# The value product of the last attention layer turned round, and the planner's lengths refreshed

## The chip, the cores and the metric

The kernel runs on one core of a Trainium2 chip. The metric is the device time of one execution in microseconds (us); the time of a kernel is the median of several executions. A profile is one more execution, recorded by the hardware. The engines have short names in it: PE is TensorE (matmuls; PEld its weight loads), DVE is VectorE, ACT is ScalarE, POOL is GpSimd, SP is the queue that issues DMAs. Everything here is float32 except the masks, which are bfloat16.

## The reference

A batch is a graph of 512 nodes with 256 features; there are 32 batches and one 512x512 adjacency matrix for all. Four layers follow one another, each of the form `x = x + layer(relu(layernorm(x)))`:

- layer 0: an MLP of width 512, graph attention without a mask (512 wide), a second MLP, graph attention with the adjacency mask (256 wide);
- layer 1: graph attention, mask with the diagonal added;
- layer 2: a transformer block with eight-head attention and the mask;
- layer 3: graph attention with four heads of 64 features, which is the layer that changes:

```python
q = (h @ W).reshape(B, N, H, D)                    # H = 4, D = 64
e = e_src[:, :, None, :] + e_dst[:, None, :, :]
e = jnp.where(e >= 0, e, ALPHA * e)
e = jnp.where(mask, e, NEG_INF)
attn = jax.nn.softmax(e, axis=2)                   # over the neighbours j
h_prime = jnp.einsum('bijh,bjhd->bihd', attn, q)
return jax.nn.elu(h_prime.reshape(B, N, H * D))
```

A node without neighbours has the same score for all nodes, so its row of `h_prime` is the mean of `q`.

## The kernel before

**Tiling.** A batch's 512 nodes are four blocks (`NC`) of 128 partitions; a feature map is either nodes first (128 partitions x 4 blocks x 256) or transposed, channels first (128 partitions x 2 x 512). Whole batches are the unit of parallel work: up to `IN_FLIGHT` = 4 of them are open, each with one of four "x" buffers that it holds from the load of its input to the store of its output.

**Order.** Nothing runs in program order. Each batch (`Graph`) first states its work as operations: an engine, a length in us, buffers read and written, and a function that issues the instructions. `Plan.order` (L158) then goes through all operations of all batches like a simulator of the five engines: it places next the operation that can start first, and among those that can start at the same time the one with the earliest due time, which is the batch's number times `PERIOD` less the length of what follows it in the batch. The result is one fixed order per engine; each engine executes its queue strictly in that order, and waits where an operand isn't there. The lengths thus decide the order and nothing else; a wrong length doesn't cost time by itself, but puts an instruction ahead of another that would have been ready sooner. `HOP` and `DRAIN` (L124) are added between engines.

**Buffers.** Work buffers are 28 of the kind "cell" (one feature map, or half of an attention matrix: two of its four 128-row blocks), 9 of the kind "row" (128 x 522) and eight PSUM banks (128 x 512). The planner assigns them as it goes, and `safe` (L231) refuses to hand one out where some batch could then not finish.

**Graph attention** is the same for all layers, in `gat_probabilities` (L587). The score is built transposed: neighbours j on the partitions, nodes i along the columns. TensorE spreads a column of node terms over all partitions by transposing it (`rows_ps`, L576); VectorE takes the masked maximum (L609) and two small steps on four columns (L618, L627, L628); TensorE and ScalarE make a row of the result (L576, L584); GpSimd adds the transposed mask to that row, two blocks at a time (L643, 128x1024); VectorE takes the maximum of the two slopes of the leaky ReLU (L655); and ScalarE takes the exponential (L663). The result p is two cells, unnormalized.

**Layer 3** is `layer3` (from L1239). `nodes_first` (L560) computes q and the 16 columns of node terms; ScalarE copies q into a cell where each head has 64 features and a 65th column that GpSimd sets to one (L1271). `lonely` (L669) computes the mean for nodes without neighbours and puts it, or zero, into y. Then each head by itself gets its p, and the value product of L1290: for each block c of 128 nodes, p's 128x128 block is loaded as the weights, and 128 columns of q that include the head's 65 stream through, four matmuls in a chain; the 65th column gives the sum of the row. VectorE clamps and inverts the sums (L1303, L1304) and adds the scaled 64 columns into y (L1306, one instruction per block). At the end ELU and the addition to x (L707, L711, L720, L1034).

The MHA of layer 2 (`mha`, L1136) already has a value product of another shape (L1206): the values are the weights, 32 columns for each of four heads, each head at its own quarter of the PSUM partitions, and p transposed streams through; the result, channels first, is copied to a row (L1219) and turned by two transposes (L1227).

Of the kernel before, what the change touches and what calls it, by code (L numbers as in the profile page):

```python
# [115 lines left out]
class Plan:  # L116
# [9 lines left out]

    def __init__(self):
        self.ops = []
        self.writers = {}
        self.readers = {}  # L130

    def add(self, graph, engine, length, reads, writes, emit, lag):
        op = Op()
        op.engine, op.length, op.emit, op.graph, op.lag = engine, length, emit, graph, lag
# [174 lines left out]
def adj_preln_kernel(  # L309
# [116 lines left out]
    def weight(w):  # L426
        return held("w", name_of[id(w)])
# [7 lines left out]
    class Graph:  # L435
# [29 lines left out]
        def normalized(self, src, func, n):  # L465
# [5 lines left out]
            for c in range(NC):  # L471
# [8 lines left out]
                "dve", 0.3, [mv], [var], lambda: dve.tensor_add(var.ap, mv[:, :, 1], eps)  # L480
            )
            self.op(
                "pool", 1.21, [var], [rstd],
# [3 lines left out]
                "dve", 0.25, [mv, rstd], [off],  # L487
# [41 lines left out]
        def channels_first(self, src, w, cols, dst, bias=None):  # L529

            nk = w.shape[1]
            for m in range(2 * len(dst)):
                mm = Buffer("bank", N)
                for k in range(nk):
                    s, i = src[k // 2], k % 2
                    self.op(
                        "pe", 0.92, [s.part(i)] if k else [*src, weight(w)],
# [16 lines left out]
        def nodes_first(self, src, w, cols, n, c, mm, dst):  # L554
# [13 lines left out]
            self.op("pe", 0.435 * nk, [*src, weight(w), terms(w)], [mm, dst], emit)  # L568
# [18 lines left out]
        def gat_probabilities(self, holder, term, n, bias=None, biasT=None, own=False, after=()):  # L587
# [10 lines left out]
            if bias is None:  # L598
# [5 lines left out]
                self.op("dve", 1.6, [f2_ps, *holder], [top, s], emit)  # L604
            else:
                for c in range(NC):
                    self.op(
                        "dve", 0.79, [f2_ps, held("mask", c)], [top],
                        lambda c=c: dve.tensor_tensor_reduce(  # L609
                            masked, f2_ps.ap, bias[:, c, :], 1.0, LOWEST,  # L610
                            op0=ALU.add, op1=ALU.max, accum_out=top[:, c : c + 1],
                        ),
                    )
# [8 lines left out]
                self.op("dve", 0.65 if own else 0.5, [top, *holder], [top, s], emit)  # L622
# [9 lines left out]
            self.op("dve", 0.8, [s, *holder], [m, w], emit)  # L632
# [36 lines left out]
        def lonely(self, v, n, y, split):  # L669
# [7 lines left out]
            self.op("pool", 1.94, [v], [add], emit)  # L677
# [23 lines left out]
        def elu(self, y, parts, shape, twice=False):  # L701
# [4 lines left out]
                "dve", 0.9 if big else 0.51, [parts], [e],  # L706
# [207 lines left out]
        def layer0(self):  # L914
# [30 lines left out]
            for i in range(2):  # L945
                self.op(
                    "pool", 1.38, [p[i]], [sums.part(i)],
# [20 lines left out]
            for m in range(KH):  # L968
# [17 lines left out]
                if i:  # L986
                    self.elu(lambda y=y: y.ap, y.part(), (2, N), twice=True)
                    self.op(
                        "pool", 2.35, [y, r1T[m // 2]], [y],
# [11 lines left out]
            for g in range(2):  # L1001
# [5 lines left out]
                def emit(g=g, tp=tp):  # L1007
# [10 lines left out]
                    "dve", 1.3, [tp, part], [part],  # L1018
# [3 lines left out]
                    "dve", 0.85, [xt.part(2 * g, 2), part], [xt.part(2 * g, 2)],  # L1022
# [97 lines left out]
        def pair_first(self, src, w, cols, c, mm, i, dst):  # L1120
# [13 lines left out]
            self.op("pe", 0.435 * nk + 0.07, [src, weight(w)], [mm.part(i), dst], emit)  # L1134

        def mha(self, g, qT, kT, v, y):  # L1136
# [7 lines left out]
            for c0 in range(0, NC, 2):  # L1144
                pT = [Buffer("cell", NC, 2, P) for _ in range(PACK)]
                for c in (c0, c0 + 1):
# [17 lines left out]
                    self.op("pe", 1.2, reads, [*sc, *p], emit)  # L1164
                    for h in range(PACK):
# [3 lines left out]
                            "dve", 0.83, [sc[h], held("mask", c)], [half, low],  # L1169
# [46 lines left out]
                self.op("pe", 2.1, [v, reads], [acc, r, valued], emit)  # L1216
# [23 lines left out]
                self.op("dve", 0.7, [back, sums], [rinv, y], emit)  # L1240

        W3 = GAT_DIM + 1

        def layer3(self):
            w3 = self.W3
            xn = self.normalized(self.xt, AF.Relu, 1)
            hT = self.transposed(xn)
            q = Buffer("cell", NC, GAT_HEADS * w3)
            f = self.small("f16", NC, TERMS, GAT_HEADS)
            n = C + TERMS * GAT_HEADS  # L1250

            def heads_of(ap):
                return ap.rearrange("p (h d) -> p h d", h=GAT_HEADS)

            for c in range(NC):
# [3 lines left out]
                def emit(c=c, mm=mm):  # L1259
# [3 lines left out]
                    act.activation(  # L1263
                        heads_of(q[:, c, :])[:, :, :GAT_DIM], heads_of(mm[:, :C]), AF.Copy
                    )

                self.op("act", 0.57, [mm], [f, q.part(c)], emit)

            def emit():
                ones_at = q.ap.rearrange("p c (h d) -> p (c h) d", h=GAT_HEADS)  # L1270
                pool.memset(ones_at[:, :, GAT_DIM:], 1.0)  # L1271

            self.op("pool", 0.13, [], [q], emit)
            y = Buffer("cell", NC, C)
            self.lonely(q, GAT_HEADS * w3, y, GAT_HEADS)
            after = []
            for h in range(GAT_HEADS):
                p, top = self.gat_probabilities(
                    [f], lambda t, h=h: f[:, :, t, h], h % 2, mask_bias, mask_biasT, False, after
                )  # L1280
                after = [top]

                first = min(h * w3, GAT_HEADS * w3 - P)
                at = h * w3 - first
                mm = Buffer("bank", NC, P)
                for c in range(NC):

                    def emit(c=c, p=p, mm=mm, first=first):
                        for j in range(NC):
                            pe.matmul(  # L1290
                                mm[:, c, :],
                                p[j // 2][:, j % 2, c * P : (c + 1) * P],
                                q[:, j, first : first + P],
                                start=(j == 0),
                                stop=(j == NC - 1),
                            )

                    self.op("pe", 1.02, [q, y.part(c), *p], [mm], emit)
                rinv = self.small(f"rinvh{h % 2}", NC, 1)

                def emit(h=h, mm=mm, rinv=rinv, at=at):
                    hs = slice(h * GAT_DIM, (h + 1) * GAT_DIM)
                    dve.tensor_max(rinv.ap, mm[:, :, at + GAT_DIM : at + w3], tiny[:, :, None])  # L1303
                    dve.reciprocal(rinv.ap, rinv.ap)  # L1304
                    for c in range(NC):
                        dve.scalar_tensor_tensor(  # L1306
# [76 lines left out]
```

## Time and profile before

Three executions took 5247.51, 5250.43 and 5252.19 us, so the median is 5250.43. The profiled execution took 5251.43 us; its span, from the first to the last instruction, is 5249.7 us.

| engine | busy, us | share of the span | instructions |
|---|---|---|---|
| PE (matmul) | 4933.7 | 94% | 28816 |
| PEld (weight loads) | 3494.5 | 67% | 28816 |
| DVE | 3652.2 | 70% | 9752 |
| ACT | 3389.3 | 65% | 7173 |
| POOL | 2222.0 | 42% | 1487 |

The rows of the parts that change:

| line, what | count | mean, ns |
|---|---|---|
| L1290 PE matmul record, 128x128 (two records make one float32 matmul) | 4096 | 282 |
| L1303 DVE clamp, 128x4 | 128 | 157 |
| L1304 DVE reciprocal, 128x4 | 128 | 178 |
| L1306 DVE scale and add, 128x64 | 512 | 277 |
| L1263 ACT copy of q, 128x256 | 128 | 382 |
| L1271 POOL ones, 128x16 | 32 | 127 |
| L643 POOL mask addition, 128x1024 | 320 + 64 | 2151, 2195 |
| L990 POOL addition, 128x1024 | 64 | 2476 |
| L948 POOL addition, 128x512 | 64 | 1284 |

A matmul's recorded length includes the time in which its last columns run out of the array while the next one already streams, so records overlap and their lengths don't add up; a transpose of 128x128 is one record. The granted TensorE clock is 0.98 of full speed over the span. DMA moves 45.58 MB in all and is busy only at the start (weights) and at each batch's load and store.

### The profile page before, as it was taken

How to read it: one execution, taken by the hardware profiler on the slowest of the kernel's cores; microseconds unless marked ns; L12 is line 12 of the kernel's file. 1: busy time of each engine (PE TensorE's matmuls, PEld its weight loads, DVE VectorE, ACT ScalarE, POOL GpSimd, SP SyncE). 2: the span in 40 equal slices, each digit the busy share in tenths (PEclk: the TensorE clock that was granted, in tenths of full speed). 3: DMA queues.
4: the chain of work that ended last, by engine and by line, in shares of the span. 5: the costliest groups of instructions: out<-in, count | busy, mean ns of one | idle time of the engine just before them, and what ended most of it. 6: DMA issues, size and time to landing. Idle time of an engine off the chain costs nothing.

```text
span 5249.7 us, 78394 instructions
## 1 busy us (share of the span) xinstructions
PE 4933.7 (94%) x28816; PEld 3494.5 (67%) x28816; DVE 3652.2 (70%) x9752; ACT 3389.3 (65%) x7173; POOL 2222.0 (42%) x1487
## 2 busy tenths in 40 slices
PE   8999999999999999999999999999999999999987
PEld 5666666676666666766666666666666666666565
DVE  5576667677767766677667767677676767767677
ACT  4656666666667666666656666666766666657774
POOL 2244444354433444343444434444344443343355
PEclk9999999999999999999999999999999999999997
DMA  2000000000000000000000000000000000000000
GB/s 70 1 9 1 9 9 9 9 9 1 9 9 9 9 1 9 9 9 9 9 1 9 9 9 9 1 9 9 9 9 1 9 9 9 9 1 9 1 5 13
DMA packets 40624, 45.58 MB, mean 9 GB/s; under 512 B 2992, under 2 KB 38320, under 8 KB 40240
## 3 DMA queue, kind: packets, MB, share of 16 engines
q1 hardware_dynamic: 38624, 40.57, 2.4%
q8 instruction: 227, 3.72, 0.3%
q14 instruction: 157, 1.29, 0.1%
q10 hardware_dynamic: 1616, 0.01, 0.0%
HBM read 23.80 MB, written 16.78 MB: 8 GB/s over the span
## 4 chain that ended last, share of the span: by engine, by line
PE 70%; DVE 18%; ACT 7%; POOL 3%; issue 2%; DMA 0%; DVEq 0%; POOLq 0%; ACTq 0%
PE bank L560 14%; PE bank L539 10%; PE bank L751 8%; PE bank L975 8%; PE bank L1290 7%; PE bank L1188 6%; PE bank L576 4%; PE bank L1206 3%; DVE masked L609 3%; PE bank L1151 3%; PE bank L1126 3%; DVE cell L655 2%; PE bank L511 2%; DVE smalls L627 2%; ACT cell L1178 1%
## 5 line engine op out<-in xcount | busy, mean ns | idle before, releaser
L643 POOL TENSOR_TENSOR cell<-mask_biasT,row 128x1024 f32<-128x1024 bf16 x320 | 681.3, 2151 | 604.0 <-ACT row L584 587.9
L1178 ACT ACTIVATE cell<-cell,smalls 128x512 f32<-128x512 f32 x1024 | 733.9, 717 | 273.1 <-DVE smalls L1170 270.2
L1170 DVE CUSTOM_DVE_ANT_0 cell<-bank,mask_bias 128x512 f32<-128x512 f32 x1024 | 684.3, 682 | 182.4 <-PE bank L1151 180.8
L609 DVE CUSTOM_DVE_ANT_0 masked<-bank,mask_bias 128x512 f32<-128x512 f32 x768 | 529.4, 689 | 395.6 <-PE bank L576 371.8
L1197 ACT ACTIVATE cell<-bank 128x512 f32<-128x512 f32 x1024 | 578.3, 593 | 218.8 <-PE bank L1188 214.6
L1188 PE MATMUL bank<-ident,cell 128*128 128x128 f32 x4096 | 588.1, 278 | 91.7 <-ACT cell L1178 49.7
L1188 PEld LDWEIGHTS bank<-ident,cell 128*128 128x128 f32 x4096 | 471.2, 142 | 261.7 <-ACT cell L1178 116.5
L1290 PEld LDWEIGHTS bank<-cell,cell 128*128 128x128 f32 x4096 | 517.4, 196 | 93.0 <-issue 65.1
L1290 PE MATMUL bank<-cell,cell 128*128 128x128 f32 x4096 | 562.4, 282 | 15.0 <-ACT cell L663 8.6
L751 PE MATMUL bank<-cell,cell 128*128 128x261 f32 x2048 | 502.0, 397 | 27.9 <-ACT cell L663 16.3
L663 ACT ACTIVATE cell<-cell,smalls 128x512 f32<-128x512 f32 x640 | 427.1, 715 | 124.7 <-DVE cell L655 123.8
L539 PE MATMUL bank<-cell,mlp_sb 128*128 128x512 f32 x1024 | 485.9, 604 | 4.3 <-ACT cell L519 3.5
L484 POOL TENSOR_TENSOR smalls<-smalls,neg_half 128x4 f32<-128x4 f32 x192 | 205.8, 1072 | 662.6 <-DVE smalls L480 495.5
L751 PEld LDWEIGHTS bank<-cell,cell 128*128 128x128 f32 x2048 | 392.2, 196 | 135.7 <-ACT cell L663 39.7
L560 PE MATMUL bank<-fc_sb,cell 128*128 128x256 f32 (+1 forms) x2048 | 480.6, 382 | 0.9 <-ACT cell L1197 0.2
L975 PE MATMUL bank<-cell,cell 128*128 128x512 f32 x1024 | 459.9, 594 | 0.0
L1034 POOL TENSOR_TENSOR x<-x,cell 128x512 f32<-128x512 f32 x192 | 259.8, 1365 | 465.8 <-DVE cell L720 426.4
L576 PE MATMUL bank<-ident,smalls 128*128 128x128 f32 x2304 | 355.2, 281 | 71.6 <-DVE smalls L628 54.4
L560 PEld LDWEIGHTS bank<-fc_sb,cell 128*128 128x128 f32 x2048 | 376.8, 191 | 59.0 <-issue 6.1
L655 DVE SCALAR_TENSOR_TENSOR cell<-bank,smalls,cell 128x512 f32<-128x512 f32 x512 | 356.2, 745 | 46.4 <-POOL cell L643 39.6
L576 PEld LDWEIGHTS bank<-ident,smalls 128*128 128x128 f32 x2304 | 270.4, 140 | 174.3 <-issue 93.4
L496 ACT ACTIVATE cell<-x,smalls 128x256 f32<-128x256 f32 x512 | 269.6, 590 | 142.8 <-DVE smalls L488 142.5
(131 smaller groups left out, 8871.9 us busy)
## 6 DMA issues: line engine op xcount, KB each, us to landing
x<-in_x_dram SPq DMA_DIRECT2D x32, 512.0 KB, 3.7
out_dram<-x SPq DMA_DIRECT2D x32, 512.0 KB, 3.0
mlp_sb<-in_L_gnn_mlp_w_dram SPq DMA_DIRECT2D x2, 512.0 KB, 6.6
fc_sb<-in_L_gnn_W_fc_dram SPq DMA_DIRECT2D x1, 1024.0 KB, 7.7
row<-in_adj_dram SPq DMA_DIRECT2D x4, 256.0 KB, 7.4
qkv_sb<-in_L_gnn_w_qkv_dram SPq DMA_DIRECT2D x1, 768.0 KB, 7.5
cell<-in_L_gnn_a_fc_dram SPq DMA_DIRECT2D x1, 512.0 KB, 6.3
l_sb<-in_L_gnn_W_dram SPq DMA_DIRECT2D x2, 256.0 KB, 5.9
```

The lines of the kernel that those rows point to most:

```text
L539: lambda k=k, s=s, i=i, m=m, mm=mm: pe.matmul(mm.ap, w[:, k, cols + m * P : cols + (m + 1) * P], s[:, i, :], start=(k == 0), stop=(k == nk ...
L560: pe.matmul(mm[:, :n], src[k // 2][:, k % 2, c * P : (c + 1) * P], w[:, k, cols : cols + n], start=(k == 0), stop=(k == nk - 1),)
L576: pe.transpose(bc[:, c * P : (c + 1) * P], col(c).to_broadcast([P, P]), ident)
L609: lambda c=c: dve.tensor_tensor_reduce(masked, f2_ps.ap, bias[:, c, :], 1.0, LOWEST, op0=ALU.add, op1=ALU.max, accum_out=top[:, c : c + 1],),
L643: lambda half=half: pool.tensor_add(p[half].ap, biasT[:, 2 * half : 2 * half + 2, :], w_row[:, None, :].to_broadcast([P, 2, N]),),
L751: pe.matmul(mm[:, :w1], p[j // 2][:, j % 2, c * P : (c + 1) * P], v[:, j, :], start=(j == 0), stop=(j == NC - 1),)
L975: pe.matmul(mm.ap, h1[jh][:, i, m * P : (m + 1) * P], p[jh][:, i, :], start=(jh + i == 0), stop=(jh + i == 2),)
L1170: lambda h=h, c=c, sc=sc, p=p: dve.tensor_tensor_reduce(p[h // 2][:, h % 2, :], sc[h].ap, mask_bias[:, c, :], -MHA_SCALE, HIGHEST, op0=ALU ...
L1178: lambda h=h, c=c, p=p: act.activation(p[h // 2][:, h % 2, :], p[h // 2][:, h % 2, :], AF.Exp, scale=-1.0, bias=low[:, c, h : h + 1], accu ...
L1188: pe.transpose(tp[:, j, :], p[h // 2][:, h % 2, j * P : (j + 1) * P], ident)
L1197: lambda h=h, c=c, tp=tp, pT=pT: act.activation(pT[h][:, :, c % 2, :], tp.ap, AF.Copy),
L1290: pe.matmul(mm[:, c, :], p[j // 2][:, j % 2, c * P : (c + 1) * P], q[:, j, first : first + P], start=(j == 0), stop=(j == NC - 1),)
```

## The change

Layer 3's heads are taken in pairs. q's 64 columns of a head become the weights, the first head of a pair on columns 0 to 63 of the array and the second on 64 to 127, and p streams through as it lies, all 512 nodes at once; the result is channels first (two heads x 64 on the partitions, nodes along the columns). The ones column goes; GpSimd adds the four blocks of each head's p to one 128x512 map instead (an addition of 128x1024, then one of 128x512), and a product with 32 columns of ones per head sums these over the partitions, the four heads at the four quarters of one bank. ScalarE copies each of the three banks to a row, TensorE turns each by four transposes, VectorE clamps and inverts the sums and multiplies, two heads at a time, into a new cell z. y, the part of the nodes without neighbours, is added last, in two halves. A head's value product no longer waits for y.

Apart from this, some twenty of the planner's lengths are set to other values, and the planner gets a new term, `OVERLAP`: operations of ScalarE and VectorE keep their engine for 0.115 and 0.07 us less than their length, and that time is added to the delay with which their result counts as there.

```diff
+    OVERLAP = {"act": 0.115, "dve": 0.07}
...
-        op.engine, op.length, op.emit, op.graph, op.lag = engine, length, emit, graph, lag
+        over = self.OVERLAP.get(engine, 0.0)
+        op.engine, op.length, op.lag = engine, length - over, lag + over
+        op.emit, op.graph = emit, graph
...
-                "pool", 1.21, [var], [rstd],
+                "pool", 1.07, [var], [rstd],
...
-                        "pe", 0.92, [s.part(i)] if k else [*src, weight(w)],
+                        "pe", 0.88, [s.part(i)] if k else [*src, weight(w)],
...
-            self.op("pe", 0.435 * nk, [*src, weight(w), terms(w)], [mm, dst], emit)
+            self.op("pe", 0.45 * nk, [*src, weight(w), terms(w)], [mm, dst], emit)
...
-                        "dve", 0.79, [f2_ps, held("mask", c)], [top],
+                        "dve", 0.77, [f2_ps, held("mask", c)], [top],
...
-                    "pool", 1.38, [p[i]], [sums.part(i)],
+                    "pool", 1.7, [p[i]], [sums.part(i)],
...
-                    "dve", 1.3, [tp, part], [part],
+                    "dve", 0.77, [tp, part], [part],
...
-            self.op("pe", 0.435 * nk + 0.07, [src, weight(w)], [mm.part(i), dst], emit)
+            self.op("pe", 0.43 * nk + 0.04, [src, weight(w)], [mm.part(i), dst], emit)
...
-                    self.op("pe", 1.2, reads, [*sc, *p], emit)
+                    self.op("pe", 1.14, reads, [*sc, *p], emit)
...
-                            "dve", 0.83, [sc[h], held("mask", c)], [half, low],
+                            "dve", 0.77, [sc[h], held("mask", c)], [half, low],
...
-                self.op("pe", 2.1, [v, reads], [acc, r, valued], emit)
+                self.op("pe", 1.97, [v, reads], [acc, r, valued], emit)
...
-                self.op("dve", 0.7, [back, sums], [rinv, y], emit)
+                self.op("dve", 1.0, [back, sums], [rinv, y], emit)
...
-            q = Buffer("cell", NC, GAT_HEADS * w3)
+            q = Buffer("cell", NC, C)
...
-                pool.memset(ones_at[:, :, GAT_DIM:], 1.0)
...
-            self.lonely(q, GAT_HEADS * w3, y, GAT_HEADS)
+            self.lonely(q, C, y, 1)
...
-                            pe.matmul(
-                                mm[:, c, :],
-                                p[j // 2][:, j % 2, c * P : (c + 1) * P],
-                                q[:, j, first : first + P],
-                                start=(j == 0),
-                                stop=(j == NC - 1),
-                            )
-
-                    self.op("pe", 1.02, [q, y.part(c), *p], [mm], emit)
...
-                    dve.tensor_max(rinv.ap, mm[:, :, at + GAT_DIM : at + w3], tiny[:, :, None])
-                    dve.reciprocal(rinv.ap, rinv.ap)
...
-                        dve.scalar_tensor_tensor(
-                            y[:, c, hs], mm[:, c, at : at + GAT_DIM], rinv[:, c, :], y[:, c, hs],
-                            op0=ALU.mult, op1=ALU.add,
-                        )
...
+                    halves = Buffer("cell", 2, N)
+                    self.op(
+                        "pool", 2.4, p, [halves],
+                        lambda p=p, halves=halves: pool.tensor_add(halves.ap, p[0].ap, p[1].ap),
+                    )
+                    self.op(
+                        "pool", 1.27, [halves], [total.part(i)],
+                        lambda i=i, halves=halves, total=total: pool.tensor_add(
+                            total[:, i, :], halves[:, 0, :], halves[:, 1, :]
+                        ),
+                    )
...
+                acc = Buffer("bank", N)
+                r = Buffer("row", N)
+                for half in range(2):
+
+                    def emit(g=g, ps=ps, acc=acc, half=half):
+                        for k in range(2):
+                            for i in range(2):
+                                d = (2 * g + i) * GAT_DIM
+                                pe.matmul(
+                                    acc[i * GAT_DIM : (i + 1) * GAT_DIM, :],
+                                    q[:, 2 * half + k, d : d + GAT_DIM],
+                                    ps[i][half][:, k, :],
+                                    start=(half + k == 0),
+                                    stop=(half + k == 2),
+                                )
+
+                    self.op("pe", 1.78, [q, ps[0][half], ps[1][half]], [acc, r], emit)
+                self.op(
+                    "act", 0.6, [acc], [r],
+                    lambda acc=acc, r=r: act.activation(r.ap, acc.ap, AF.Copy),
+                )
...
+                for h in range(GAT_HEADS):
+                    d = slice(h * 32, (h + 1) * 32)
+                    pe.matmul(
+                        acc[d, :], ones[:, d], sums[h // 2][:, h % 2, :], start=True, stop=True
+                    )
+
+            self.op("pe", 0.94, sums, [acc, r], emit)
...
+                    for c in range(NC):
+                        pe.transpose(back[:, c, :], r[:, c * P : (c + 1) * P], ident)
+
+                self.op("pe", 0.5, [r, *dst], [back, *dst], emit)
...
+                dve.tensor_scalar_max(
+                    rinv.ap, back.ap.rearrange("p c (h d) -> p c h d", d=32)[:, :, :, 0], TINY
+                )
+                dve.reciprocal(rinv.ap, rinv.ap)
+
+            self.op("dve", 0.35, [back], [rinv], emit)
...
+                    dve.tensor_mul(
+                        z[:, :, g * P : (g + 1) * P].rearrange("p c (h d) -> p c h d", h=2),
+                        back.ap.rearrange("p c (h d) -> p c h d", h=2),
+                        rinv[:, :, 2 * g : 2 * g + 2, None].to_broadcast([P, NC, 2, GAT_DIM]),
+                    )
+
+                self.op("dve", 0.72, [back, rinv], [z], emit)
...
+                    lambda s=s: dve.tensor_add(z[:, s, :], z[:, s, :], y[:, s, :]),
...
+            self.elu_to_xt(z)
```

The lengths of `elu`, `lonely`, the small steps of `gat_probabilities` and of `normalized`, and of two additions in layer 0 move in the same way, by up to 0.2 us.

## The prediction

> **What bounds the kernel now.** I read the first page, then the chain of waits, then the timeline of TensorE in a middle stretch. The page:
>
> ```profile
> span 5249.7 us, 78394 instructions
> PE 4933.7 (94%) x28816; PEld 3494.5 (67%) x28816; DVE 3652.2 (70%) x9752; ACT 3389.3 (65%) x7173; POOL 2222.0 (42%) x1487
> ...
> PE 70%; DVE 18%; ACT 7%; POOL 3%; issue 2%; DMA 0%; DVEq 0%; POOLq 0%; ACTq 0%
> ```
>
> TensorE leads both lists. But its busy time counts the draining end of each matmul, so I price TensorE by pitch, from one start to the next.
>
> ```profile
> 2734.13 1.05 PE L1290 MATMUL bank<-cell,cell 128*128 128x128 f32 x8
> 2735.02 0.60 PE L576 MATMUL bank<-ident,smalls 128*128 128x128 f32 x4
> 2735.45 1.06 PE L1290 MATMUL bank<-cell,cell 128*128 128x128 f32 x8
> ...
> 2749.75 1.93 PE L1206 MATMUL bank<-cell,cell 128*32 128x256 f32 x32
> 2751.61 1.16 PE L1290 MATMUL bank<-cell,cell 128*128 128x128 f32 x8
> ```
>
> This is the timeline of TensorE: start, length, line, shape, count. Eight records of L1290 (four f32 matmuls of two passes each) take 2735.02 - 2734.13 = 0.89 us. Four transposes of L576 take 0.43, so 0.109 a record. L1206 (MHA's value product, four heads on 32-column groups) puts 32 records of 256 columns into 1.86 us.
>
> The chain in order of time gives the pitch of the widest form, and the period:
>
> ```profile
> 2615.43 5.24 DMA x<-in_x_dram
> ...
> 2843.44 5.15 PE bank L975 x12
> 2848.59 7.06 PE bank L751 x32
> ...
> 3262.72 3.68 DMA x<-in_x_dram
> ```
>
> L975's 512-column records have a pitch of 5.15/12 = 0.429 us; L751's of 261 columns 0.221. An x buffer is loaded again after 647.3 us, that is four batches, so a batch takes 161.8 us. Per batch TensorE issues (counts of the page and the group view over 32): 272 transposes x 0.109 = 29.6; 64 of L1290 x 0.112 = 14.3; 64 of L751 x 0.221 = 14.1; 88 of 512 columns x 0.429 = 37.8; 144 of 256 to 272 columns x 0.22 = 31.5; eight score units at 1.07 = 8.6; four L1206 units at 1.86 = 7.4; small ones 1.8. Sum 145.1 of 161.8: TensorE bounds, with 16.7 us (10%) of idle and drains per batch.
>
> **What the Trainium skill says.** "Trainium Kernel Development and Optimization", Performance Expectations, calls matmul busy time a bad metric, since matmuls are pipelined; the trace agrees, 94% by busy time, 90% by pitch. "TensorEngine Tiling (Array Packing)", Tiling Modes, lists 128x64 as two tiles that execute independently, and says that a change of mode drains the engine. No record of before is 64 columns wide; for 32 the trace agrees: L1206's 16 matmuls would take 16 x 0.44 = 7.0 us one by one and take 1.86, against 4 x 2 x 0.215 = 1.72 for perfect fours (half of L975's 0.429 below), so 0.14 us of entry per unit. "SBUF — State Buffer", Who interferes with whom, says that a DVE instruction with two SBUF inputs and a GpSimd instruction that reads SBUF exclude each other. The trace agrees, in the timeline of the last 45 us:
>
> ```profile
> 5205.03 4.21 POOL L643 TENSOR_TENSOR cell<-mask_biasT,row 128x1024 f32<-128x1024 bf16 x2
> ...
> 5205.55 1.62 DVE L618 SCALAR_TENSOR_TENSOR smalls<-smalls 128x4 f32<-128x4 f32 x1
> 5207.21 2.05 DVE L627 SCALAR_TENSOR_TENSOR smalls<-smalls 128x4 f32<-128x4 f32 x1
> ...
> 5209.60 1.94 PE L576 MATMUL bank<-ident,smalls 128*128 128x128 f32 x8 [5.22 <-DVE smalls L628]
> ```
>
> Two DVE instructions on four columns, 0.16 us by their median, stretch to the end of one GpSimd addition each, and TensorE waits 5.22 us.
>
> **The change, per batch.**
>
> TensorE, removed: 16 units of L1290 x 0.89 = 14.3 us. They streamed 128 columns per query block and kept 65.
> Added: four units, each of four 512-wide matmuls in two pairs. Side by side a pair takes one matmul's 2 x 0.429 = 0.858, a unit 1.72; with L1206's entry 1.86, so 7.4. The ones product has four 32-column matmuls of 512: 0.858 + 0.14 = 1.0. Three turns of four transposes: 12 x 0.109 = 1.3. Together 9.7, saving 4.6 us (5.2 if no entry is paid).
>
> VectorE, removed: 4 x (0.157 + 0.178 + 4 x 0.277) = 5.8 (rows of L1303, L1304, L1306). Added: clamp and reciprocal 0.34; two multiplications out of PSUM at L984's 0.686 = 1.4; two additions of SBUF pairs, bounded by L720's shortest 0.656 and mean 0.770, taken at 0.7 = 1.4. Net 2.7 saved, worth nothing directly: VectorE has 30% idle.
>
> ScalarE, added: three evictions at L1197's 0.593 = 1.8 us. Free while the following turns aren't urgent; exposed, the last serial part of a batch only.
>
> GpSimd, removed: a memset of 0.13, which also stood ahead of the isolated-node sum; the value product loses its wait for that sum's result. Added: per head one addition of 1024 columns (L990's median 2.36, mean 2.48; take 2.42) and one of 512 (L948's 1.28), so 4 x 3.7 = 14.8 us. GpSimd goes from 2222 to about 2222 + 32 x 14.7 = 2690 us, 51%. Behind these additions in its queue stand L643 (for which DVE L655, the exponentials and the next value product wait) and the rstd powers of L484. What covers this now:
>
> ```profile
> POOL cell L643 <- ACT row L584: 715.0, 156, 29.7
> ...
> DVE cell L655 <- POOL cell L643: 76.0, 69, 7.3
> ```
>
> In the list of waits GpSimd waits 715 us for rows, and VectorE only 76 us for GpSimd. The exclusion grows too: mean minus median of L627 (533 - 164 ns, 224 times), L480, L618, L628 and the shorter L707 sums to some 280 us over the run; with GpSimd busy 1.21 times as long, +59 us on VectorE. The chain is 18% VectorE, so I put 10 us on the path; the bounds are 0 and 59.
>
> Buffers: a pair of heads holds q, y, four p, a total and a halves, eight cells, up to nine with the first pair's total, where single heads overlapping held about six. MHA's own stage holds about eleven. I take no cost from 28 cells; a shortage would show as TensorE idle, and is in the first rival.
>
> The end: the last head's units and DVE part (5230.4 to 5241) become addition, ones, eviction, turn, clamp, turns and sums; by the rows above 2 us longer.
>
> The lengths move no work, only the order. Before, the planner reserves 155.5 us of TensorE per batch (its lengths summed over the code) where the trace needs 145.1; after, 147.0 where I count 140.5. The excess falls from 10.4 to 6.5 us. If idle follows the excess, that is 3.9 x 32 = 125 us; if order is chance, nothing, or a loss of like size. I take a third, 40 us.
>
> Sum, against the profiled execution (5251.43; span 5249.7 and 1.7 around it): 5251.4 - 32 x 4.6 (147) - 40 + 10 + 2 = 5076. The median shown is 1 us lower: 5075.
>
> **Rivals.**
> 1. *The time goes into idle.* Heads in pairs wait for the slower head, cells are held longer, and TensorE waits where it worked: 10 of the 147 us stay, or up to 50, so 5200 to 5240. For: 10% idle already. Against: four batches in flight, and VectorE and ScalarE at 70% or less.
> 2. *GpSimd's queue decides, and it is slower.* Six pairs of L643 per batch each find half an addition (1.2 us) ahead, uncovered: 6 x 1.2 = 7.2 against 4.6 gained, 2.6 x 32 = +83 us, about 5335. It decides from 4.6/6 = 0.77 us per pair. Against: the 715 us above.
> 3. *The change doesn't do what it says.* If 64-column halves run one after the other: 16 x 0.858 + 4 x 0.14 + 2.3 = 16.6 against 14.3, +73 us, 5324. It breaks even at a packing gain of 13.7/12.0 = 1.14. L1206 speaks against it.
> 4. *The refreshed order takes all its excess out*: 5251 - 147 - 125 = about 4980.
>
> **How the numbers follow.** Main case 0.62 (its own range 5020 to 5160), rival 1 0.13, rival 2 0.06, rival 3 0.04, rival 4 0.15. A measurement tells 0.2% (10 us) from no change: rival 1 gives 0.10 to faster and 0.03 to same, rivals 2 and 3 are the slower, so faster 0.87, same 0.03, slower 0.10. The range reaches down to 4960, rival 4 with its 20 us of slack, and up to 5215, the better half of rival 1; left out are rivals 2 and 3 (0.10) and the other half of 1 (0.07).
>
> **What would show it.** 28816 - 32 x 76 = 26384 matmul records; a new unit's pitch near 1.86 us (3.4 if rival 3); the ones product near 1.0; GpSimd near 2690 us, VectorE near 3630, ScalarE near 3446; the reload period near 4 x 156 us. Waits of L655 for L643 far above 76 us would speak for rival 2; those numbers right with the same time, for rival 1. A period much under 155 means that the order, not the value product, gave more.

## The result, and the profile after

The changed kernel takes 5251.98 us (median of 12) beside 5250.70 of the kernel before (12): a ratio of the means of 1.0005, 95% interval 0.9996 to 1.0014. Nothing was gained or lost; 5075 us was forecast.

The first page after, with the lines that answer to those of before (span; busy time by engine; the chain of waits by engine):

```profile
span 5250.2 us, 73401 instructions
PE 4845.9 (92%) x26384; PEld 3125.2 (60%) x26384; DVE 3705.8 (71%) x9176; ACT 3438.9 (65%) x7269; POOL 2688.1 (51%) x1711
...
PE 19%; DVE 10%; ACT 4%; POOL 2%; issue 1%; POOLq 0%; DVEq 0%; ACTq 0%
```

The counts are as forecast: 26384 matmul records, GpSimd at 2688 us, ScalarE at 3439. VectorE is at 3706 us, 76 above the forecast. The chain adds up to little over a third of the span (the trace loses it further back), so its shares aren't compared with those of before.

The new units, in TensorE's timeline after (start, length, line, shape, count):

```profile
2236.59 0.65 PE L580 MATMUL bank<-ident,smalls 128*128 128x128 f32 x4 [1.72 <-DVE smalls L632]
...
2238.93 1.94 PE L1299 MATMUL bank<-cell,cell 128*64 128x512 f32 x8
2240.80 1.14 PE L1155 MATMUL bank<-cell,cell 32*128 32x512 f32 x8
...
1929.73 1.06 PE L1320 MATMUL bank<-cell,ones 128*32 128x512 f32 x8
1930.72 1.09 PE L1192 MATMUL bank<-ident,cell 128*128 128x128 f32 x8
```

A value unit takes 2240.80 - 2238.93 = 1.87 us and the ones product 0.99: the heads do run side by side, and TensorE saves its 4.6 us per batch. So the work went and the time stayed.

Where it stayed can be read from the stores of the batches (the queue of SP): the first, the 27th of 32, and the last four, merged. Before, then after:

```profile
368.01 0.40 SPq L1324 DMA_DIRECT2D out_dram<-x  x1
...
4550.97 0.38 SPq L1324 DMA_DIRECT2D out_dram<-x  x1
...
5090.71 155.40 SPq L1324 DMA_DIRECT2D out_dram<-x  x4
```

```profile
396.76 0.40 SPq L1381 DMA_DIRECT2D out_dram<-x  x1
...
4500.38 0.38 SPq L1381 DMA_DIRECT2D out_dram<-x  x1
...
5038.92 207.76 SPq L1381 DMA_DIRECT2D out_dram<-x  x4
```

The first store comes 28.8 us later. From it, 26 batches take 160.9 us each before and 157.8 after: 79.3 us gained. From the 27th store to the end of the last one, five batches, it is 5246.1 - 4551.0 = 695.1 before and 746.3 after: 51.2 lost. The three terms, 28.8 - 79.3 + 51.2, leave 0.7 us.

The lists of waits of before and of after, for TensorE (matmul and weight load) waiting for the last of the four-column steps ahead of it, and for the mask additions:

```profile
PE bank L576 <- DVE smalls L628: 54.4, 41, 5.2
...
PEld bank L576 <- DVE smalls L628: 29.1, 21, 3.3
```

```profile
POOL cell L647 <- ACT row L588: 476.1, 142, 22.5
...
PEld bank L580 <- DVE smalls L632: 126.0, 49, 10.0
...
PE bank L580 <- DVE smalls L632: 124.0, 60, 9.7
...
DVE cell L659 <- POOL cell L647: 55.9, 43, 4.7
```

VectorE doesn't wait longer for GpSimd's mask additions (55.9 us, 76.0 before). What grew is TensorE's wait for a VectorE step of 0.16 us: 54.4 to 124.0 us for matmuls. (The weight loads' list can count the same gap again, so the two aren't added.)

### The profile page after: what moved, and what is told of

Read it like the earlier page. It is cut to its first block, busy times and chain, and to the rows that moved or that the text cites. A ratio compares the mean times of both kernels' runs of the same rounds, so it can differ in the third digit from the quotient of the medians.

```text
span 5250.2 us, 73401 instructions
## 1 busy us (share of the span) xinstructions
PE 4845.9 (92%) x26384; PEld 3125.2 (60%) x26384; DVE 3705.8 (71%) x9176; ACT 3438.9 (65%) x7269; POOL 2688.1 (51%) x1711
## 5 line engine op out<-in xcount | busy, mean ns | idle before, releaser
L1182 ACT ACTIVATE cell<-cell,smalls 128x512 f32<-128x512 f32 x1024 | 736.7, 720 | 238.8 <-DVE smalls L1174 236.6
L647 POOL TENSOR_TENSOR cell<-mask_biasT,row 128x1024 f32<-128x1024 bf16 x320 | 683.6, 2157 | 377.7 <-ACT row L588 369.6
L1192 PE MATMUL bank<-ident,cell 128*128 128x128 f32 x4096 | 612.5, 283 | 114.9 <-ACT cell L1182 64.2
L667 ACT ACTIVATE cell<-cell,smalls 128x512 f32<-128x512 f32 x640 | 444.2, 721 | 162.5 <-DVE cell L659 155.8
L564 PE MATMUL bank<-fc_sb,cell 128*128 128x256 f32 (+1 forms) x2048 | 491.4, 386 | 4.0 <-DVE smalls L1174 2.5
L580 PE MATMUL bank<-ident,smalls 128*128 128x128 f32 x2304 | 364.5, 288 | 139.0 <-DVE smalls L632 124.0
L755 PEld LDWEIGHTS bank<-cell,cell 128*128 128x128 f32 x2048 | 381.6, 192 | 118.0 <-ACT cell L667 23.6
L1038 POOL TENSOR_TENSOR x<-x,cell 128x512 f32<-128x512 f32 x192 | 272.7, 1436 | 280.0 <-DVE cell L724 239.1
L715 ACT ACTIVATE cell<-cell 128x512 f32<-128x512 f32 (+1 forms) x256 | 184.4, 733 | 262.6 <-DVE cell L711 262.3
L1281 POOL TENSOR_TENSOR cell<-cell,cell 128x1024 f32<-128x1024 f32 x128 | 302.1, 2368 | 51.7 <-ACT cell L667 26.5
```

Of the source, the lines that this page charges most:

```text
L564: pe.matmul(mm[:, :n], src[k // 2][:, k % 2, c * P : (c + 1) * P], w[:, k, cols : cols + n], start=(k == 0), stop=(k == nk - 1),)
L580: pe.transpose(bc[:, c * P : (c + 1) * P], col(c).to_broadcast([P, P]), ident)
L647: lambda half=half: pool.tensor_add(p[half].ap, biasT[:, 2 * half : 2 * half + 2, :], w_row[:, None, :].to_broadcast([P, 2, N]),),
L667: lambda j=j, ph=ph, i=i: act.activation(ph[:, i, :], ph[:, i, :], AF.Exp, bias=term(1)[:, j : j + 1]),
L755: pe.matmul(mm[:, :w1], p[j // 2][:, j % 2, c * P : (c + 1) * P], v[:, j, :], start=(j == 0), stop=(j == NC - 1),)
L1182: lambda h=h, c=c, p=p: act.activation(p[h // 2][:, h % 2, :], p[h // 2][:, h % 2, :], AF.Exp, scale=-1.0, bias=low[:, c, h : h + 1], accu ...
```

## The experiments

Each is compared with the kernel before, run beside it; the median of that was between 5248.7 and 5253.1 us. Differences from it are taken against its own value.

| run | us | ratio to before, 95% interval |
|---|---|---|
| value product alone | 5408 | 1.0293 (1.0278 to 1.0309) |
| lengths alone | 5144 | 0.9791 (0.9777 to 0.9806) |
| after, small additions | 5138 | 0.9782 (0.9767 to 0.9796) |
| after, first addition doubled | 5420 | 1.0314 (1.0297 to 1.0331) |
| after, memsets for additions | 5160 | 0.9820 (0.9805 to 0.9835) |
| after, one-column steps | 5122 | 0.9750 (0.9736 to 0.9765) |
| lengths alone, one-column steps | 5079 | 0.9668 (0.9652 to 0.9684) |
| after, small additions, planned | 5162 | 0.9824 (0.9810 to 0.9839) |
| before, half of the value product | 5189 | 0.9879 (0.9864 to 0.9894) |
| lengths, one-column steps, half of the value product | 5025 | 0.9570 (0.9556 to 0.9585) |
| after, small additions, one-column steps | 5078 | 0.9673 (0.9657 to 0.9690) |
| after, one-column steps, half of the units | 5107 | 0.9725 (0.9710 to 0.9739) |
| before, VectorE's step halved | 5220 | 0.9941 (0.9925 to 0.9958) |
| before, ScalarE's eviction halved | 5228 | 0.9961 (0.9949 to 0.9973) |
| OVERLAP alone | 5167 | 0.9840 (0.9825 to 0.9854) |
| lengths without OVERLAP | 5195 | 0.9893 (0.9878 to 0.9907) |

### The two halves of the change

Layer 3 of after in the kernel before, every other length kept, and the reverse.

```diff
# before.py
-        (layer3 and W3 of before)
+        (layer3 of after, its own lengths with it)
```

> The new value product in the kernel before: layer 3 as after, every other length and the planner as before (no OVERLAP). Theory A (the refreshed lengths made an order that loses what the value product gains): 5090 to 5140 us. Theory B (GpSimd's new additions shut VectorE's small steps out and stand in GpSimd's queue): 5220 to 5280, since the additions are all here. Theory C (the heads in pairs and the longer chain after them cost the gain at the start and the end of the run, where no other batch fills in): 5220 to 5270 too.

5408 us: 155 us slower than before (5253), worse than every theory said.

```diff
# after.py
-        (layer3 of after)
+        (layer3 and W3 of before)
```

> The refreshed lengths and OVERLAP alone, layer 3's value product as before. Theory A: 5340 to 5400 us, slower than before by what the value product gained. Theory B and C: 5200 to 5260, the lengths near nothing or a small gain.

5144 us: 109 us faster, better than any theory said. So the change is two effects of opposite sign. The refreshed lengths gain 109 us; on top of them the new value product, with 147 us less of TensorE, loses 5252 - 5144 = 108. The order changes with it, so the 108 is not the work of its instructions alone. Theory A falls: it had the signs the wrong way round.

### GpSimd's additions, in one order

The order depends on the lengths in the plan only. If these stay, an operation can be made shorter or longer in the same order.

```diff
-lambda p=p, halves=halves: pool.tensor_add(halves.ap, p[0].ap, p[1].ap),
+lambda p=p, halves=halves: pool.tensor_add(
+    halves[:, :, :16], p[0][:, :, :16], p[1][:, :, :16]
+),
...
-total[:, i, :], halves[:, 0, :], halves[:, 1, :]
+total[:, i, :16], halves[:, 0, :16], halves[:, 1, :16]
```

> The changed kernel in the same order, with the two GpSimd additions per head of layer 3 cut from 512 to 16 columns per block, so the sums of the rows are left out for the other columns (that part of the result is not computed). GpSimd falls from 2688 to some 2250 us busy. Theory B: most of the missing gain comes back, 5100 to 5160 us, and the mean of the four-column VectorE steps falls back to 330 to 600 ns. Theory A and C: 5225 to 5250.

5138 us: the additions cost 114 us, of GpSimd time that no engine seemed to wait for. The page of that run, and the wait that had grown:

```profile
PE 4795.3 (93%) x26384; PEld 3104.5 (60%) x26384; DVE 3580.2 (70%) x9176; ACT 3435.0 (67%) x7269; POOL 2284.0 (44%) x1711
...
PE bank L580 <- DVE smalls L632: 72.2, 40, 9.7
```

```diff
-lambda p=p, halves=halves: pool.tensor_add(halves.ap, p[0].ap, p[1].ap),
+lambda p=p, halves=halves: [
+    pool.tensor_add(halves.ap, p[0].ap, p[1].ap) for _ in range(2)
+],
```

> The changed kernel in the same order, with the 1024-column addition of each head of layer 3 issued twice (the second writes the same values). GpSimd 2688 + 302 = 2990 us. Theory B: slower again by a like dose, 302/466 of the loss, so 5320 to 5350 us. Theory A and C: 5250 to 5275.

5420 us: 168 us more for 302 us of GpSimd, beyond the 5320 to 5350 expected and a steeper dose than the 114 for the first 404 (2688 - 2284). Theory B stands (A and C expected no such effect), but it has two halves: the additions stand in GpSimd's queue, and they exclude VectorE's instructions with two SBUF inputs. As far as the waits tell, the second dose came mainly by the queue. VectorE is busy only 25 us more (3731), TensorE's wait for L632 is what it was after the change (124.0), and VectorE's wait for the mask additions has doubled (55.9):

```profile
PE bank L580 <- DVE smalls L632: 123.5, 62, 9.7
...
DVE cell L659 <- POOL cell L647: 111.4, 57, 10.8
```

To part the two in the first dose, memsets can take the place of the additions: a memset on GpSimd takes time and reads nothing.

```diff
-lambda p=p, halves=halves: pool.tensor_add(halves.ap, p[0].ap, p[1].ap),
+lambda p=p, halves=halves: [
+    pool.memset(halves.ap, 1.0), pool.memset(halves.ap, 1.0),
+    pool.memset(halves[:, 0, :], 1.0),
+],
...
-pool.tensor_add(total[:, i, :], halves[:, 0, :], halves[:, 1, :])
+[pool.memset(total[:, i, :], 1.0), pool.memset(total[:, i, :], 1.0)]
```

> The changed kernel in the same order, with memsets of ones in place of layer 3's two GpSimd additions per head, repeated to take a like time on GpSimd but reading nothing (the sums of the rows are thus left out, and with them the right scale of the result). GpSimd again near 2690 us busy. Theory B1 (the additions cost by shutting out VectorE's instructions with two SBUF inputs, as a reading GpSimd does): 5130 to 5170 us, VectorE busy near 3590. Theory B2 (they cost by standing in GpSimd's queue ahead of the mask additions and the x additions): 5230 to 5260 us.

5160 us, with GpSimd as busy as in the changed kernel. Its page, and the four-column steps in its list of groups (busy us, mean ns; then idle before):

```profile
PE 4814.7 (93%) x26384; PEld 3110.7 (60%) x26384; DVE 3596.5 (70%) x9176; ACT 3438.7 (67%) x7269; POOL 2661.5 (52%) x2095
...
L622 DVE SCALAR_TENSOR_TENSOR smalls<-smalls 128x4 f32<-128x4 f32 x128 | 117.6, 919 | 2.6
L631 DVE SCALAR_TENSOR_TENSOR smalls<-smalls 128x4 f32<-128x4 f32 x224 | 115.7, 517 | 2.6
...
L632 DVE SCALAR_TENSOR_TENSOR smalls<-smalls 128x4 f32<-128x4 f32 x160 | 54.9, 343 | 5.5
```

And the same groups after the change:

```profile
L631 DVE SCALAR_TENSOR_TENSOR smalls<-smalls 128x4 f32<-128x4 f32 x224 | 145.4, 649 | 2.8 <-issue 0.2
L622 DVE SCALAR_TENSOR_TENSOR smalls<-smalls 128x4 f32<-128x4 f32 x128 | 116.9, 914 | 2.9 <-DVE smalls L613 0.5
...
L632 DVE SCALAR_TENSOR_TENSOR smalls<-smalls 128x4 f32<-128x4 f32 x160 | 111.5, 697 | 5.5
```

With memsets 5160 - 5138 = 22 us of the loss stay, and 5252 - 5160 = 92 go. L632, which TensorE waits for, falls from 697 to 343 ns, as with the small additions (331). L622 stays at 0.9 us: of its 98 long instances in that trace (over 0.3 us), 76 end as a mask addition of another attention (L647) ends, and that reads too.

The split into 22 and 92 isn't clean. A memset reads no p, so it doesn't wait for the exponentials either, as the additions do. The additions after the change, then the memsets (busy us, mean ns; then idle before):

```profile
L1281 POOL TENSOR_TENSOR cell<-cell,cell 128x1024 f32<-128x1024 f32 x128 | 302.1, 2368 | 51.7 <-ACT cell L667 26.5 <-issue 12.5 <-PE bank L1192 2.4
```

```profile
L1282 POOL MEMSET cell<- 128x1024 f32 x256 | 244.1, 954 | 14.9 <-PE bank L1302 3.5 <-PE bank L1192 2.5 <-PE bank L1155 1.6
```

So the 22 us hold GpSimd's time without that wait at the head of its queue, and the 92 are an upper figure for reading.

The other way round, the additions stay and the steps lose their second SBUF tensor, with the lengths in the plan unchanged:

```diff
-dve.scalar_tensor_tensor(m.ap, s.ap, ALPHA, s.ap, op0=ALU.mult, op1=ALU.max)
+for c in range(NC):
+    k = slice(c, c + 1)
+    dve.tensor_scalar(m[:, k], s[:, k], ALPHA, s[:, k], op0=ALU.mult, op1=ALU.max)
...
(likewise s from top and term(0), and w from term(0) and m)
```

> The changed kernel with its additions, in the same order (lengths in the plan unchanged), where the three four-column steps of each attention's probabilities are issued as twelve one-column steps whose second operand is a per-partition scalar, so that they have one SBUF input and no reason to wait for GpSimd. Twelve at about 0.07 to 0.1 us are near the 0.5 us of the three. Theory B1: 5120 to 5180 us. Theory B2: 5240 to 5280.

5122 us, 130 less than the changed kernel.

```profile
L635 DVE TENSOR_SCALAR smalls<-smalls 128x1 f32<-128x1 f32 x896 | 127.1, 204 | 0.3
...
L640 DVE TENSOR_SCALAR smalls<-smalls 128x1 f32<-128x1 f32 x640 | 90.8, 204 | 0.0
```

Each one-column step takes 204 ns on average, here and in the next run, which has 464 us less of GpSimd. The reading on GpSimd's side and the second SBUF tensor on VectorE's have now each been taken away, and the time falls each time. This is as the Trainium skill has it ("SBUF — State Buffer", Who interferes with whom): a VectorE instruction with at most one SBUF input, outside the modes in which it uses two ports, doesn't contend with GpSimd, and one with two inputs doesn't contend with a GpSimd instruction that only writes.

> The refreshed lengths with the old value product (5144 us) and the same one-column steps. The steps there lose some (560 - 164) x 224 + (529 - 166) x 128 + (371 - 163) x 160 ns = 169 us of VectorE to the mask additions. Theory B1: 5060 to 5110 us. Theory B2: 5130 to 5170.

The same edit with the old value product: 5079 us. The steps had cost 65 us there, by the GpSimd work that the kernel already had, and so in all likelihood in the kernel before, where the exclusion was on view. This kernel computes everything and beats both: 0.9668 (0.9652 to 0.9684).

> The changed kernel with the one-column steps (5122 us) and with layer 3's GpSimd additions cut to 16 columns (the sums of the other columns left out), same order. If what is left of the loss still comes from the additions (through VectorE's ELU steps and GpSimd's queue): 5030 to 5070 us. If the additions no longer cost once the small steps are free of them: 5100 to 5120, and what is missing lies in the order, the pairs and the longer end.

5078 us (edits as above), between the two ranges, nearer the first. Once the steps are free, the additions still cost 5122 - 5078 = 44 us, about twice what was left with the memsets (22). VectorE is 3640 us busy with the additions and 3588 with the small ones. Most of that difference is one step, once per batch, which adds the row's maximum in layer 0's attention without a mask. With the additions, then with the small ones:

```profile
L606 DVE TENSOR_SCALAR smalls<-smalls 128x4 f32<-128x4 f32 x32 | 44.9, 1403 | 1.9
```

```profile
L606 DVE TENSOR_SCALAR smalls<-smalls 128x4 f32<-128x4 f32 x32 | 13.1, 409 | 1.9
```

It has one SBUF tensor and a per-partition scalar, as the new steps have, but four columns, and it is still stretched (its median is 0.23 us). VectorE's ELU steps add about 15 us. What the 44 us are made of was not tried.

### What a saved microsecond of TensorE is worth

Without the additions' effects, the new value product (5078) equals the old one (5079), and yet TensorE has 147 us less to do. So I cut TensorE's work and nothing else, in the order of the kernel before:

```diff
-                            for j in range(NC):
+                            for j in (0, NC - 1):
                                 pe.matmul(
                                     mm[:, c, :],
```

> The kernel before in its order, with two of the four neighbour blocks left out of layer 3's value product (j = 0 and 3 stay, so every wait stays; half of the sum is not computed). TensorE loses 64 records x 0.112 x 32 batches = 229 us and nothing else changes. It measures what saved TensorE time is worth. Theory T (TensorE bounds, as the prediction had it: one for one or more): 5020 us or less. Theory D (the fixed order and the waits between engines bound; saved TensorE time mostly becomes idle): 5130 to 5200.

5189 us: of 229 us of TensorE work, 62 came out as time, 27%. The page of that run:

```profile
PE 4790.0 (93%) x26768; PEld 3306.5 (64%) x26768; DVE 3666.7 (71%) x9752; ACT 3385.8 (65%) x7173; POOL 2221.8 (43%) x1487
```

TensorE still shows 93%, with 64 x 32 = 2048 records fewer: the busy share hides what was saved.

> The same cut (229 us of TensorE, half of the value product's sum left out) in the kernel with the refreshed lengths and the one-column steps, old value product, 5079 us. Theory T: 4850 us. Theory D: 4960 to 5030.

The same edit on the 5079 us kernel: 5025, 54 of 229 us, 24%.

```diff
-                        for k in range(2):
+                        for k in range(1):
...
-                                    start=(half + k == 0),
-                                    stop=(half + k == 2),
+                                    start=(half == 0),
+                                    stop=(half == 1),
```

> The changed kernel with the one-column steps (5122 us), same order, with one of two blocks left out in each unit of the new value product (half of the sum is not computed; every wait stays). TensorE loses 16 records x 0.215 x 32 = 110 us. Theory T: 5010 us. Theory D: 5060 to 5100.

With the new units: 5107, 16 of 110 us, 14%, just beyond the 5060 to 5100 of theory D. Theory T fails three times; theory D has the kind right three times and the range twice.

Not all of the rest went into waiting. The granted clock fell too. Before, then with half of the value product:

```profile
core 0: 5249.7 us, clock 0.980
```

```profile
core 0: 5177.8 us, clock 0.971
```

What it does can be seen behind the wait of 5.22 us that the prediction shows. Between 5212 and 5218 us the granted clock is 0.50:

```profile
5211.99 7.01 PE L1290 MATMUL bank<-cell,cell 128*128 128x128 f32 x32 [0.44 <-ACT cell L663]
...
5218.84 0.60 PE L576 MATMUL bank<-ident,smalls 128*128 128x128 f32 x4
```

A record takes (5218.84 - 5211.99)/32 = 0.214 us there, against 0.112. The clock that wasn't granted, times the span, is an upper estimate of what TensorE loses so, as it is idle for a part of that time: 0.020 x 5250 = 105 us before, 0.029 x 5178 = 150 in the cut kernel. Thus up to 45 of the 167 us that didn't come out were TensorE itself working more slowly. In the other two cuts (0.991 to 0.981, and 0.977 to 0.972) it is up to 50 of 175 and up to 25 of 94. The clock was lower in every run whose TensorE work was cut; what lowers it was not tried.

Is another engine the bound, then? The same test for two of them:

```diff
-                        ph[:, i, :], f1_ps.ap, term(3)[:, j : j + 1],
-                        w_row.ap if biasT is None else ph[:, i, :],
+                        ph[:, i, :n], f1_ps[:, :n], term(3)[:, j : j + 1],
+                        w_row[:, :n] if biasT is None else ph[:, i, :n],
(n is 256 where there is a mask)
```

> The kernel before in its order, with VectorE's maximum-and-add of the masked attentions (640 instructions of 512 columns) run on 256 columns, the scores of the other half left without that step. At some 0.745 - 0.42 us each VectorE loses about 208 us. What is saved VectorE time worth, beside TensorE's 62 of 229 us? If the chains between engines set the pace, an engine at 70% on those chains is worth as much as TensorE at 90%: 5160 to 5210 us. If TensorE's queue alone does: 5230 to 5255.

```diff
-                                pT[h][:, :, c % 2, :], tp.ap, AF.Copy
+                                pT[h][:, 0:2, c % 2, :], tp[:, 0:2, :], AF.Copy
```

> The kernel before in its order, with ScalarE's eviction of MHA's transposed probabilities (1024 instructions of 512 columns) run on two of four blocks, the other two not copied. At 0.593 - 0.382 us each ScalarE loses 216 us. If the chains set the pace: 5160 to 5210 us. If TensorE's queue alone does: 5230 to 5255.

5220 and 5228 us. VectorE's busy time fell by 206 us and the time by 29 (14%); ScalarE's by 185 and the time by 21 (11%). Both miss the 5160 to 5210 of theory D, and the 5230 to 5255 of its rival too. In the same order, a microsecond of these two is worth about half of TensorE's or less, and TensorE's only a quarter; GpSimd's additions, with 114 us for 404, were worth as much as TensorE's work. So no engine is the bound by itself: in a fixed order with four open batches, most of an engine's saved time turns into waiting for the others or, for TensorE, into a lower clock. The granted clock was the same here (0.979 and 0.980).

### The order

> The kernel with the additions cut to 16 columns (sums of the other columns left out), now with lengths of 0.25 and 0.2 us for them in the plan, so that the order no longer keeps GpSimd's time free for them. It was 5138 us with the order of the changed kernel. If the order made for the additions is what still hides the 4.6 us per batch that TensorE saves: 4980 to 5060 us. If the pairs and the longer chain hide it (theory C): 5110 to 5150.

```diff
-                        "pool", 2.4, p, [halves],
+                        "pool", 0.25, p, [halves],
...
-                        "pool", 1.27, [halves], [total.part(i)],
+                        "pool", 0.2, [halves], [total.part(i)],
```

5162 us, 24 slower than the same short additions in the order made for long ones. Both ranges missed, and knowing the true length didn't help. So two orders of the same work can differ by 24 us, without a reason that was found.

> The kernel before with the planner's OVERLAP term alone (0.115 and 0.07 us of ScalarE's and VectorE's lengths turned into delay), every length as before. The refreshed lengths with OVERLAP are at 5144 us. If the order gained because the planner had taken ScalarE and VectorE for fuller than they are: most of the 109 us, 5150 to 5190. If it gained by TensorE's and GpSimd's lengths: 5230 to 5270.

```diff
+    OVERLAP = {"act": 0.115, "dve": 0.07}
...
+        over = self.OVERLAP.get(engine, 0.0)
+        op.engine, op.length, op.lag = engine, length - over, lag + over
...
```

> The refreshed lengths without the OVERLAP term, old value product. If OVERLAP carries the gain: 5230 to 5280 us. If the lengths carry it: 5150 to 5190.

```diff
-    OVERLAP = {"act": 0.115, "dve": 0.07}
+    OVERLAP = {}
```

5167 and 5195 us: OVERLAP alone gains 82 us, as expected, the lengths alone 53 (5248.7 - 5195.4), between the two ranges, and both 109. OVERLAP carries most of it, the two don't add up, and why an order is better was not looked into further.

## Why the prediction was wrong

**TensorE's prices** were right: 1.87 us a unit (1.86 forecast), 0.99 for the ones product (1.0), every count.

**The sum's main term failed.** The step was "TensorE bounds, with 16.7 us (10%) of idle", and so 32 x 4.6 = 147 us one for one. TensorE's work did go, and cuts of it were worth 27%, 24% and 14%. The prediction also priced every record at the full clock. The granted clock went from 0.980 to 0.969 with the change, so by the same upper estimate (0.031 x 5250 - 0.020 x 5250) up to 58 us of the 147 went there. (In its list, "64 of L1290" should be 128 records; the 14.3 us beside it are for 128.) What the saving came to can be read in a pair. These are the stores of two kernels with the old and the new value product, one-column steps in both, the additions cut in the second; their orders differ too:

```profile
387.52 0.40 SPq L1336 DMA_DIRECT2D out_dram<-x  x1
...
4378.96 0.38 SPq L1336 DMA_DIRECT2D out_dram<-x  x1
...
4909.66 162.45 SPq L1336 DMA_DIRECT2D out_dram<-x  x4
```

```profile
389.25 0.40 SPq L1391 DMA_DIRECT2D out_dram<-x  x1
...
4342.72 0.38 SPq L1391 DMA_DIRECT2D out_dram<-x  x1
...
4873.41 190.52 SPq L1391 DMA_DIRECT2D out_dram<-x  x4
```

153.5 us a batch with the old value product, 152.1 with the new: 38 us over 26 batches, a third of the 26 x 4.6 = 120 that were priced. From the store at 4379 to the end it is 693.1, from that at 4343 it is 721.2: 28 us go back at the end, where no new batch fills in. The prediction had 2 us there. After the very last exponential the end is 5 us longer (20.6 us after the change, 15.4 before). The clock can have a part in the rest: over these last five batches it is 0.95 with the old value product and 0.91 with the new, in this pair and in before and after alike, which is up to some 30 us by the estimate above. That the pairs and the longer chain in each of the last batches make TensorE idle there is argued, not shown.

**The exclusion was mis-sized.** The prediction showed it, with TensorE waiting 5.22 us behind it, summed its VectorE time to 59 us by proportion, and put 10 us on the path, as the chain's 18% share. The additions cost 114 us, outside the bounds of 0 and 59; at most 92 of it by reading, the rest by GpSimd's queue. Two things were too small. The VectorE time itself: 126 us more than with the small additions (3706 and 3580), not 59. And its share on the path: a blocked step doesn't cost its own length, it holds VectorE's queue and the transposes that wait for its four columns. In the same order, TensorE's matmuls waited 72 us for L632 with the small additions and 124 with the full ones, and the granted clock went from 0.978 to 0.969.

**The order gained 109 us**, where a third of 125 was guessed; by itself it was near the 125 of rival 4. That it came so near is luck: the 125 were worked out from TensorE's lengths, and OVERLAP, which changes none of them, had no term and gained 82 us alone.

The steps from one kernel to the other, by the runs: 5253 before, 5144 with the refreshed lengths, 5138 with the new value product but small additions, 5252 with the additions. The middle step is worth 6 us where 147 were priced. It changes the order as well, and two orders of the same work were 24 us apart, so the value product's own worth isn't known better than that.

**The rivals.** Rival 1 had the outcome in kind, not its size: it kept 10 to 50 us, and gave the pairs as the reason, which hold at most for the end. What it was held down by, four batches in flight, didn't keep TensorE fed. Rival 2 blamed the additions' place in the queue; its mark, longer waits of L655 for L643, didn't come with the change, and came when the additions were doubled (111.4 us). Rival 3 fell with the unit's 1.87 us. A cell shortage was not tried.

## What to carry to other kernels

An engine that is busiest need not be the bound: cut some of its work in the unchanged order and see what comes out before pricing a change at one for one, and compare the granted clocks of the two runs. GpSimd work isn't free just because nothing seems to wait for it; look for VectorE instructions with two SBUF inputs whose mean is far above their median, and who waits for them. Give such steps a per-partition scalar for the second operand, one column at a time, and test the two halves of a combined change apart.

## What the runs showed of the hardware that was not expected

A VectorE step of 128x4 that takes 0.16 us alone had a mean of 0.3 to 0.9 us in these kernels, beside GpSimd's additions. As four one-column instructions with a per-partition scalar it takes 127.1/896 x 4 = 0.57 us of busy time on average (L635), slower alone than the one it replaces, and the kernel is 65 to 130 us faster for it. A four-column step with a per-partition scalar (L606) was still stretched, to 1.4 us on average.

Behind one long wait the granted TensorE clock was 0.50, and a record of the value product took 0.214 us in place of 0.112. Over the whole run the granted clock was 0.980 before the change and 0.969 after it, though TensorE had less to do.
